# Row turns on the whole TensorE array and in other groups, and small tasks behind the score maxima, in a transformer block with an expert layer

## The chip, the cores and the metric

The kernel runs on one core of a Trainium2 chip. The metric is the device time of one execution in microseconds (us); of several executions the median is given.

A core has a matrix engine (TensorE, PE in the profile, with its weight loads shown as PEld), a vector engine (VectorE, DVE), a scalar engine (ScalarE, ACT), a general one (GpSimd, POOL) and one that here only issues transfers (SyncE, SP). Each works through its own list of instructions, and they wait for each other by semaphores. TensorE writes to a memory of its own, PSUM, from which VectorE and ScalarE take results ("evict" them).

## The reference

The input is 8 batches of 1,024 rows of 256 values. Cut to what matters:

```
h = layernorm(x) * (1 + ca) + sa
q, k, v = h @ w_qkv                 # 16 heads of 64
attn = softmax(q k^T / 8)           # over 1,024 keys, for each batch and head
x = x + ga * (concat(attn v) @ w_o)
h = layernorm(x) * (1 + cb) + sb
scores = softmax(h @ router_w + router_b)      # 8 experts
G, idx = top_k(scores.T, 512)                  # 512 rows for each expert
y[idx] += G * (relu(h[idx] @ w1 + b1) @ w2 + b2)
x = x + gb * y
```

The modulation vectors sa, ca, ga, sb, cb, gb come from a small product, one row for each batch. All is in 32-bit floating point.

## The kernel before

**Units and groups.** Attention is cut into 128 units. A unit is one batch, one pair of heads and one half (512) of the queries; there are 16 units in a batch. Its keys come in 8 chunks of 128. The main loop (line 732) runs over groups, numbered g, with two chunks of scores in each, so four groups make a unit and 64 make a batch. `gm = g % 4` is the place in the unit: first group (0) to last group (3).

**What a group does.** In order: loads that are due; in the second group the spreading of the previous unit's row maxima (`max_spread`); `subtract` on VectorE for two chunks of an earlier unit; for each of two chunks the scores (`scores_mm`, L367, two matmuls), a copy from PSUM by ScalarE (L376) and the running maximum on VectorE (L381); one small task, kind "m1"; VectorE and ScalarE tasks of kind "post"; the exponential on ScalarE (L429); the products with v for two chunks (`values_mm`, L438), which lag the scores by six groups; the sums of the exponentials on GpSimd (`add_up`, L454 and L457). In the last group of a unit there follow `max_turn` and `split_max`: eight transposes of the running maximum into PSUM (L388), a reduction (L396) and the splitting of the result into three short numbers (L401 to L404). Last come tasks of the kinds "pool" and "m2".

**Banks.** Scores have two PSUM buffers (pool `ps_s`), and the turned maximum takes one of the two until it is split. So the second chunk of scores in the next unit can't be written before L404 is done. Small tasks share one other buffer (`ps_m`).

**Small tasks.** Kind "m1" holds `qk_task` (L332), `v_task` (L349) and `max_rows` (L410). The first two make q, k and v for the next heads. Each of the second, third and last groups has about one of them, 1.8 us of TensorE each.

**Tasks around the attention.** `ln_task` prepares a later batch's rows, a quarter of a batch at a time: load, statistics on VectorE (`ln_stats`, L116 and L117), normalization on GpSimd (`ln_norm`, L281), and `ln_out`, which turns the rows by TensorE so that features lie across partitions, and evicts the turned rows with scale and shift. `out_load`, `out_proj` (L548) and `out_norm` (L571 to L573) do the output projection and the second normalization of the batch before, in eight parts; `out_turn` turns two parts, `out_route` (L600) makes the router's products, `out_exp` and `out_score` (L622 to L626) its softmax, `out_store` stores rows.

**Turns.** A turn of 256 rows by 256 features is four blocks of 128 by 128. Except in batch 0, `ln_out` makes each block of two matmuls with 64 columns of the rows as weights and the identity as data (L306), and so does `out_turn` (L585).

**Where tasks go.** There is no planner: `at(g, kind, ...)` puts a task into group g, and `run` takes it. `free_slot(g, True)` finds the next last group that has no such task yet; `free_slot(g)` the next second or third group. Both input turns, output turns and output projections thus stand in last groups, behind the maxima. By these calls a middle batch has, counted in groups from its start: projections in 7, 11, 19, 23, 31, 35, 59, 63; output turns in 3, 15, 27, 55; input turns in 39, 43, 47, 51. Batch 0 has only input turns, batch 1 has six projections and two output turns, and batch 7 ten and six.

**After the loop** the last batch's projection and routing follow, then the choice of rows for each expert by a search of the threshold, and the expert layer.

Of the kernel before, what the change touches and what calls it, by code (L numbers as in the profile page):

```python
# [31 lines left out]
AF = mybir.ActivationFunctionType  # L32
ALU = mybir.AluOpType
# [4 lines left out]
P = 128  # L38
# [4 lines left out]
def adaln_block(  # L43
# [15 lines left out]
    nc = tc.nc  # L59
    B, S, D = x.shape  # L60
    H, _, _, N = w_qkv.shape
    E, _, F = w1.shape
    K = 512
    KC = D // P
    NT = S // P
# [7 lines left out]
    scale = 1.0 / N**0.5  # L73
# [4 lines left out]
    ident = const.tile([P, P], F32, name="ident")  # L78
# [17 lines left out]
    modT = const.tile([P, 2 * KC, B], F32, name="modT")  # L96
# [36 lines left out]
    ps_m = attn.enter_context(tc.tile_pool(name="ps_m", bufs=1, space=PSUM))  # L133
# [33 lines left out]
    for i in range(2):  # L167
        t = work.tile([P, NT // 2, D], F32, tag="p", name=f"x_first{i}", bufs=PB)
# [73 lines left out]
    hTs, mods, qks, vs, oTs = {}, {}, {}, {}, {}  # L242
# [4 lines left out]
    def at(g, where, f, *args):  # L247
        steps.setdefault((g, where), []).append((f, args))

    def run(g, where):  # L250
        for f, args in steps.pop((g, where), ()):
            f(*args)
# [4 lines left out]
    def bank(shape, name, start=False):  # L257

        if start:
            return ps_s.tile(shape, F32, tag="s", name=name)  # L260
        return ps_m.tile(shape, F32, tag="mm", name=name)
# [24 lines left out]
    def ln_out(b, t):  # L286
        if t == 0:
            hTs[b] = work.tile([P, KC, S], F32, tag="hT", name=f"hT{b}")
        xt = ln_x.pop((b, t))[0]
        pt = bank([P, KC, 2 * P], f"ptx{b}_{t}", (b, t) in ((0, 0), (0, 1)))  # L290
        if b == 0:
            for k in range(KC):
                for i in range(2):
                    nc.tensor.transpose(
                        pt[:, k, i * P : (i + 1) * P], xt[:, i, k * P : (k + 1) * P], ident
                    )
                nc.scalar.activation(
                    hTs[b][:, k, 2 * t * P : (2 * t + 2) * P], pt[:, k, :], AF.Identity,
                    bias=modT[:, k, b : b + 1], scale=modT[:, KC + k, b : b + 1],
                )  # L300
            return
        for k in range(KC):
            for i in range(2):
                for m in range(2):
                    c0 = k * P + m * N
                    nc.tensor.matmul(  # L306
                        pt[m * N : (m + 1) * N, k, i * P : (i + 1) * P],
                        xt[:, i, c0 : c0 + N], ident, start=True, stop=True,
                    )
        for k in range(KC):  # L310
            nc.vector.tensor_scalar(
                hTs[b][:, k, 2 * t * P : (2 * t + 2) * P], pt[:, k, :],
                modT[:, KC + k, b : b + 1], modT[:, k, b : b + 1],
                op0=ALU.mult, op1=ALU.add,
            )

    def ln_task(b, t, g):
        at(g - 4, "load", ln_load, b, t)
        at(g - 2, "post", ln_stats, b, t)
        at(g - 1, "pool", ln_norm, b, t)  # L320
        at(g, "m2", ln_out, b, t)
# [70 lines left out]
    def split_max(u):  # L392

        tt = turned.pop(u)
        nm = tt[:, :2, :8]
        nc.vector.tensor_reduce(nm[:, 0, :], tt, AX.X, ALU.max, negate=True)  # L396
        part = [
            parts_of[u % 2][:, :, :, i].rearrange("p t j -> p j t") for i in range(3)
        ]
        whole, rest = (nm[:, i, :].rearrange("p (j t) -> p j t", j=2) for i in range(2))  # L400
        nc.vector.tensor_copy(part[0], whole)  # L401
        nc.vector.tensor_sub(rest, whole, part[0])
        nc.vector.tensor_copy(part[1], rest)
        nc.vector.tensor_sub(part[2], rest, part[1])  # L404
# [171 lines left out]
    def out_turn(pool, b, t, tag="mm"):  # L576

        n = f"{b}_{t}"
        pt = pool.tile([P, 2, KC, P], F32, tag=tag, name=f"pth{n}")
        for i in range(2):  # L580
            h2 = o_h[b, t + i]
            for k in range(KC):
                for m in range(2):
                    c0 = k * P + m * N
                    nc.tensor.matmul(  # L585
                        pt[m * N : (m + 1) * N, i, k, :], h2[:, c0 : c0 + N], ident,
                        start=True, stop=True,
                    )
        h2T = small.tile([P, 2, KC, P], F32, tag="h2T", name=f"h2T{n}", bufs=1)
        nc.scalar.copy(h2T, pt)  # L590
        o_x[b, t] = h2T
# [54 lines left out]
        )  # L646


    taken = set()

    def free_slot(g, behind=False):
        while g in taken or g % 4 == 0 or behind != (g % 4 == 3):
            g += 1
        taken.add(g)
        return g


    for t in range(NT // 2):
        at(-1 if t < 2 else 0, "m1", ln_out, 0, t)
        ln_task(1, t, free_slot(39 + 4 * t, True))  # L660
    for i, g in ((0, -1), (2, -1), (1, 0), (3, 1)):
        at(g, "m1", qk_task, 0, 0, i)
    for t, g in enumerate((1, 2, 3)):
# [1 line left out]
    for b in range(B):  # L665
        for p in range(NP):
            P0 = 8 * (b * NP + p)
            for i, g in enumerate((-7, -6, -5, -2)):
                if P0:
                    at(P0 + g, "m1", qk_task, b, p, i)  # L670
            if p % 2 == 0:
                for t, g in enumerate((-9, -3, -1, 5)):
                    if P0 or g > 0:
                        at(P0 + g, "m1", v_task, b, p // 2, t)
            if (b, p) == (B - 1, NP - 1):
                continue

            at(P0 + 17, "load", den_load, b, p)
            at(P0 + 18, "post", den_inv, b, p)
            at(P0 + 19, "load", den_spread, b, p)  # L680
            at(P0 + 20, "pool", den_mul, b, p)
        if b + 1 < B:
            if b + 2 < B:
                for t in range(NT // 2):
                    ln_task(b + 2, t, free_slot(64 * (b + 1) + 39 + 4 * t, True))
            for t in range(NT):
                g = free_slot(64 * (b + 1) + 19 + 4 * t, True)
                at(g - 2, "load", out_load, b, t)
                at(g, "m2", out_proj, ps_m, b, t)
                at(g + 1, "pool", out_norm, b, t)  # L690
                if t % 2:
                    g = free_slot(g + 2, True)
                    at(g, "m2", out_turn, ps_m, b, t - 1)
                    g = free_slot(g + 1)
                    at(g, "m2", out_route, ps_m, b, t - 1)
                    at(g + 1, "post", out_exp, b, t - 1)
                    at(g + 2, "post", out_score, b, t - 1)
                    at(g + 3, "pool", out_store, b, t - 1)
    for u in range(NSU):
        at(4 * u + 4, "m1", max_rows, u)  # L700
        if u < NSU - 1:
# [8 lines left out]
    with tc.manual_schedule():  # L710
# [20 lines left out]
        g = -1  # L731
        while g < 4 * NSU + LAG or steps:
            u, gm = divmod(g, 4)
            run(g, "load")
            if gm == 1 and 0 < u <= NSU:
                max_spread(u - 1)
            u1, gm1 = divmod(g - LAG + 1, 4)
            late = [(u1, 2 * gm1 + i) for i in range(2) if 0 <= u1 < NSU]

            for uc in late[: 1 if gm == 3 else 2]:  # L740
                subtract(*uc)
            if 0 <= u < NSU:
                for c in (2 * gm, 2 * gm + 1):
                    scores_out(u, c, scores_mm(u, c))
            if gm == 3 and late:
                subtract(*late[1])
            run(g, "m1")
            run(g, "post")
            for uc in late:
                exp_of(*uc)  # L750
            u1, gm1 = divmod(g - LAG, 4)
            if 0 <= u1 < NSU:
                for c in (2 * gm1, 2 * gm1 + 1):
                    values_mm(u1, c)
                    if u1 == NSU - 1:
                        if c == 0:
                            pd_last = ps_s.tile([P, QH], F32, tag="s", name="pd_last")
                        den_mm(pd_last, probs.pop((u1, c)), start=(c == 0), stop=(c == NT - 1))
                if gm1 == 3:
                    values_out(u1)  # L760
                if u1 < NSU - 1:
                    add_up(u1, gm1)
            if gm == 3 and 0 <= u < NSU:
                max_turn(u)
                split_max(u)
            run(g, "pool")
            run(g, "m2")
            g += 1


        b = B - 1
# [82 lines left out]
    with tc.tile_pool(name="search", bufs=2) as se, tc.tile_pool(  # L854
# [4 lines left out]
        for dst, pattern, mult in (  # L859
# [3 lines left out]
            i = po_.tile(list(dst.shape), I32, name=f"i_{dst.name}")  # L863
# [29 lines left out]
        for s in range(15):  # L893
            bit = 28 - 2 * s
            cnt = se.tile([P, 3], F32, tag="cnt", name=f"cnt{s}")
            for k in range(3):
# [3 lines left out]
                    op0=ALU.is_ge, op1=ALU.add, accum_out=cnt[:, k : k + 1],  # L900
# [209 lines left out]
```

## Time and profile before

| | |
|---|---|
| median of 3 runs | 3617.36 us (3617.17 to 3618.96) |
| the profiled execution | 3616.66 us |
| its span, first to last instruction | 3614.9 us |
| attention, batch 0 to batch 7 | 22 to 3185 us |
| tail of attention, search, experts | 3185 to 3615 us |
| busy in one middle batch of 398 us: PE, DVE, ACT, POOL | 396.2, 340.8, 298.4, 325.6 us |

A line of a group or of a timeline gives the engine, the line of the kernel, the operation, what it writes and reads with shapes, and a count. In a timeline the first two numbers are the start and the length in us from the start of the span, neighbouring instructions of one kind are merged (x8), and square brackets hold the idle time before it and what ended that. On TensorE an fp32 matmul is two instructions, and the ends of matmuls are modelled, so starts are the safer reading.

### The profile page before, as it was taken

To read this page: it belongs to the slowest core of one execution; us is meant where nothing else is said; L and a number is where in the kernel's file an instruction comes from. 1 tells how busy PE (TensorE), PEld (TensorE's weight loads), DVE (VectorE), ACT (ScalarE), POOL (GpSimd) and SP (SyncE) were. 2 spreads that over 40 slices of the span, in tenths; PEclk is the share of its full clock that TensorE was granted. 3 is DMA by queue.
4 is the path that set the end of the run, shared out by engine and by line. 5 is a ranking of instruction groups with operands and counts; after the bars stand their busy time and mean duration, and the time that the engine had idled before them with its cause. 6 is when DMAs were issued, how large, how long until landed. Compare 5 with 4: busy or idle time off the path is not lost. (4 is left out here: it accounts for less than half of the span.)

```text
span 3614.9 us, 54207 instructions
## 1 busy us (share of the span) xinstructions
PE 3458.4 (96%) x20622; PEld 1456.3 (40%) x20622; DVE 2898.9 (80%) x3641; ACT 2439.8 (67%) x2988; POOL 2660.0 (74%) x1537
## 2 busy tenths in 40 slices
PE   7999999999999999999999999999999999982898
PEld 3333333343433443344433434334334344342565
DVE  5888888888888888888888888888888888857442
ACT  4777777777777777777777777777777777730111
POOL 2778777887788887977888788877888877851332
PEclk9999999999999999999999999999999999995999
DMA  3010012011111113111211112011201112133332
GB/s 77 13 42 31 25 32 67 29 45 45 59 50 35 51 49 64 31 39 51 61 46 44 41 44 62 30 52 48 67 29 45 45 59 49 51 87 121 94 100 41
DMA packets 189652, 185.39 MB, mean 51 GB/s; under 512 B 48952, under 2 KB 167240, under 8 KB 189264
## 3 DMA queue, kind: packets, MB, share of 16 engines
q1 hardware_dynamic: 173616, 160.29, 15.5%
q0 software_dynamic: 7168, 12.72, 1.7%
q10 hardware_dynamic: 8608, 8.92, 0.8%
q8 instruction: 162, 2.65, 0.3%
q14 instruction: 98, 0.80, 0.1%
HBM read 127.06 MB, written 63.21 MB: 53 GB/s over the span
## 5 line engine op out<-in xcount | busy, mean ns | idle before, releaser
L457 POOL TENSOR_TENSOR acc<-acc,p 128x1024 f32<-128x1024 f32 x762 | 1806.6, 2371 | 361.2 <-ACT p L429 328.1
L376 ACT COPY p<-s 128x1024 f32<-128x1024 f32 x1024 | 997.2, 1020 | 417.8 <-PE s L367 407.7
L426 DVE TENSOR_TENSOR p<-p,less 128x1024 f32<-128x1024 f32 x1024 | 1206.8, 1210 | 32.5 <-PE less L423 30.0
L381 DVE TENSOR_TENSOR top<-top,s 128x1024 f32<-128x1024 f32 x768 | 936.9, 1220 | 276.5 <-ACT p L376 236.2
L429 ACT ACTIVATE p<-p 128x1024 f32<-128x1024 f32 x1024 | 1042.8, 1058 | 73.7 <-DVE p L426 73.4
L367 PE MATMUL s<-qk,qk 64*128 64x512 f32 x4096 | 1025.1, 612 | 34.0 <-DVE parts L404 31.0
L438 PE MATMUL av<-p,v 128*64 128x512 f32 x4096 | 967.1, 593 | 1.8 <-ACT oT L447 1.8
L367 PEld LDWEIGHTS s<-qk,qk 64*128 64x128 f32 x4096 | 358.7, 186 | 527.8 <-issue 241.2
L332 PE MATMUL pq<-hT,wq 128*64 128x512 f32 x2048 | 498.4, 608 | 2.7 <-ACT v L354 2.1
L438 PEld LDWEIGHTS av<-p,v 128*64 128x64 f32 x4096 | 280.5, 137 | 461.4 <-issue 366.2
L454 POOL TENSOR_TENSOR acc<-p,p 128x1024 f32<-128x1024 f32 x127 | 301.8, 2376 | 178.0 <-ACT p L429 178.0
L332 PEld LDWEIGHTS pq<-hT,wq 128*64 128x64 f32 x2048 | 124.8, 136 | 342.4 <-issue 210.8
L349 PE MATMUL pv<-wq,hT 128*64 128x256 f32 x2048 | 249.3, 385 | 0.7 <-ACT qk L337 0.7
L1035 ACT ACTIVATE h<-ph,b_sb 128x512 f32<-128x512 f32 x64 | 44.1, 689 | 274.7 <-PE ph L1031 274.7
L396 DVE TENSOR_REDUCE tt<-tt 128x8 f32<-128x1024 f32 x128 | 157.4, 1230 | 69.6 <-PE tt L388 69.5
L548 PE MATMUL po<-wo,ot 128*64 128x256 f32 x1792 | 205.7, 382 | 0.0
L349 PEld LDWEIGHTS pv<-wq,hT 128*64 128x64 f32 x2048 | 135.6, 136 | 153.3 <-issue 65.9
L381 DVE TENSOR_TENSOR top<-p,s 128x1024 f32<-128x1024 f32 x128 | 155.8, 1217 | 14.5 <-ACT p L376 14.5
L388 PEld LDWEIGHTS tt<-ident,top 128*128 128x128 f32 x1024 | 109.6, 140 | 106.6 <-DVE top L381 105.8
L519 POOL TENSOR_TENSOR oT<-oT,rb 128x1024 f32<-128x1024 f32 x63 | 150.1, 2382 | 3.0 <-DMA rb<-rden_d 3.0
L548 PEld LDWEIGHTS po<-wo,ot 128*64 128x64 f32 x1792 | 123.6, 137 | 66.1 <-issue 9.4
L388 PE MATMUL tt<-ident,top 128*128 128x128 f32 x1024 | 139.9, 280 | 2.6 <-DVE top L381 2.6
(166 smaller groups left out, 2357.3 us busy)
## 6 DMA issues: line engine op xcount, KB each, us to landing
rb<-rden_d SPq DMA_DIRECT2D x128, 256.0 KB
oT_d<-oT SPq DMA_DIRECT2D x62, 512.0 KB
ot<-oT_d SPq DMA_DIRECT2D x56, 512.0 KB
rows_d<-row SPq DMA_DIRECT2D x64, 132.0 KB
rows_d<-gb_d SPq DMA_DIRECT2D x8, 1024.0 KB
w<-in_L_ffn_w_dram ACTq DMA_DIRECT2D x8, 1024.0 KB
w<-in_L_ffn_w_dram SPq DMA_DIRECT2D x8, 1024.0 KB
lnx<-in_L_attn_inputs_dram SPq DMA_DIRECT2D x28, 256.0 KB
```

Source lines behind the costliest of these rows:

```text
L332: nc.tensor.matmul(pq[m * N : (m + 1) * N, :], wq_of(k, a, 2 * p + m), hTs[b][:, k, sl], start=(k == 0), stop=(k == KC - 1),)
L349: nc.tensor.matmul(pv[m * N : (m + 1) * N, i, :], hTs[b][:, k, t0 : t0 + N], wq_of(k, 2, 4 * g, 4), start=(k == 0), stop=(k == KC - 1),)
L367: nc.tensor.matmul(ps[:, j, :], kt[r, c * P : (c + 1) * P], qt[r, h * QB : (h + 1) * QB], start=True, stop=True,)
L376: nc.scalar.copy(probs[u, c], ps)
L381: nc.vector.tensor_tensor(tops[u], probs[u, 0] if c == 1 else tops[u], ps, ALU.max)
L388: nc.tensor.transpose(turned[u][:, 4 * j + t, :], top[:, j, t * P : (t + 1) * P], ident)
L426: nc.vector.tensor_tensor(probs[u, c], probs[u, c], less[u], ALU.add)
L429: nc.scalar.activation(probs[u, c], probs[u, c], AF.Exp)
L438: nc.tensor.matmul(avs[u][j * N : (j + 1) * N, :], v[:, c, hh * N : (hh + 1) * N], pT[:, j, :], start=(c == 0), stop=(c == NT - 1),)
L454: nc.gpsimd.tensor_tensor(sums[u], pts[0], pts[1], ALU.add)
L457: nc.gpsimd.tensor_tensor(sums[u], sums[u], pt, ALU.add)
L548: nc.tensor.matmul(po[m * N : (m + 1) * N, :], ot[:, p, m * N : (m + 1) * N], wo[:, p, :], start=(p == 0), stop=(p == NP - 1),)
```

## The change

There are three parts.

1. **Turns.** `ln_out` and `out_turn` make each 128 by 128 block by one `transpose` on the whole array. In `ln_out` all four come first and then two evictions, by ScalarE, for every batch. (Before, batch 0 had transposes, interleaved with evictions by ScalarE; the others had half-array matmuls and evictions by VectorE.)
2. **Places.** `free_slot` goes. Counted in groups of a batch, input turns now stand in 30, 34, 42 and 46 and output turns in 26, 38, 50 and 62: all third groups. Projections stand in 19, 23, 31, 35, 43, 47, 55 and 59, last groups. The output turn comes 3 groups after its second projection, the router's products after 6, its exponential after 7, its softmax's end after 9, the store after 10. Input rows are prepared for the next batch, with load, statistics and normalization 4, 2 and 1 groups ahead of their turn as before, which is now one batch number lower in the formula and the same batch in effect.
3. **Last groups without an output projection.** There the small task ("m1") runs after the maxima are turned and split, not before.

```diff
@@ ln_out
-        if b == 0:
-            for k in range(KC):
-                for i in range(2):
-                    nc.tensor.transpose(
-                        pt[:, k, i * P : (i + 1) * P], xt[:, i, k * P : (k + 1) * P], ident
-                    )
-                nc.scalar.activation(
...
-            return
         for k in range(KC):
             for i in range(2):
-                for m in range(2):
-                    c0 = k * P + m * N
-                    nc.tensor.matmul(
-                        pt[m * N : (m + 1) * N, k, i * P : (i + 1) * P],
-                        xt[:, i, c0 : c0 + N], ident, start=True, stop=True,
-                    )
+                nc.tensor.transpose(
+                    pt[:, k, i * P : (i + 1) * P], xt[:, i, k * P : (k + 1) * P], ident
+                )
         for k in range(KC):
-            nc.vector.tensor_scalar(
-                hTs[b][:, k, 2 * t * P : (2 * t + 2) * P], pt[:, k, :],
-                modT[:, KC + k, b : b + 1], modT[:, k, b : b + 1],
-                op0=ALU.mult, op1=ALU.add,
+            nc.scalar.activation(
+                hTs[b][:, k, 2 * t * P : (2 * t + 2) * P], pt[:, k, :], AF.Identity,
+                bias=modT[:, k, b : b + 1], scale=modT[:, KC + k, b : b + 1],
             )
@@ out_turn
-                for m in range(2):
-                    c0 = k * P + m * N
-                    nc.tensor.matmul(
-                        pt[m * N : (m + 1) * N, i, k, :], h2[:, c0 : c0 + N], ident,
-                        start=True, stop=True,
-                    )
+                nc.tensor.transpose(pt[:, i, k, :], h2[:, k * P : (k + 1) * P], ident)
@@ places
-        ln_task(1, t, free_slot(39 + 4 * t, True))
...
-            if b + 2 < B:
-                for t in range(NT // 2):
-                    ln_task(b + 2, t, free_slot(64 * (b + 1) + 39 + 4 * t, True))
+            for t in range(NT // 2):
+                ln_task(b + 1, t, 64 * b + (30, 34, 42, 46)[t])
             for t in range(NT):
-                g = free_slot(64 * (b + 1) + 19 + 4 * t, True)
+                g = 64 * (b + 1) + 19 + 4 * (t + t // 2)
+                covered.add(g)
                 at(g - 2, "load", out_load, b, t)
                 at(g, "m2", out_proj, ps_m, b, t)
                 at(g + 1, "pool", out_norm, b, t)
                 if t % 2:
-                    g = free_slot(g + 2, True)
-                    at(g, "m2", out_turn, ps_m, b, t - 1)
-                    g = free_slot(g + 1)
-                    at(g, "m2", out_route, ps_m, b, t - 1)
-                    at(g + 1, "post", out_exp, b, t - 1)
-                    at(g + 2, "post", out_score, b, t - 1)
-                    at(g + 3, "pool", out_store, b, t - 1)
+                    at(g + 3, "m2", out_turn, ps_m, b, t - 1)
+                    at(g + 6, "m2", out_route, ps_m, b, t - 1)
+                    at(g + 7, "post", out_exp, b, t - 1)
+                    at(g + 9, "post", out_score, b, t - 1)
+                    at(g + 10, "pool", out_store, b, t - 1)
@@ main loop
-            run(g, "m1")
+
+            behind = gm == 3 and g not in covered
+            if not behind:
+                run(g, "m1")
             run(g, "post")
...
             if gm == 3 and 0 <= u < NSU:
                 max_turn(u)
                 split_max(u)
+            if behind:
+                run(g, "m1")
             run(g, "pool")
             run(g, "m2")
```

More of the change, by code (lines that the diff above doesn't have):

```diff
@@ L290, in ln_out @@
         pt = bank([P, KC, 2 * P], f"ptx{b}_{t}", (b, t) in ((0, 0), (0, 1)))
-        if b == 0:
-            for k in range(KC):
-                for i in range(2):
-                    nc.tensor.transpose(
-                        pt[:, k, i * P : (i + 1) * P], xt[:, i, k * P : (k + 1) * P], ident
-                    )
-                nc.scalar.activation(
-                    hTs[b][:, k, 2 * t * P : (2 * t + 2) * P], pt[:, k, :], AF.Identity,
-                    bias=modT[:, k, b : b + 1], scale=modT[:, KC + k, b : b + 1],
-                )
-            return
         for k in range(KC):
             for i in range(2):
-                for m in range(2):
-                    c0 = k * P + m * N
-                    nc.tensor.matmul(
-                        pt[m * N : (m + 1) * N, k, i * P : (i + 1) * P],
-                        xt[:, i, c0 : c0 + N], ident, start=True, stop=True,
-                    )
+                nc.tensor.transpose(
+                    pt[:, k, i * P : (i + 1) * P], xt[:, i, k * P : (k + 1) * P], ident
+                )
         for k in range(KC):
-            nc.vector.tensor_scalar(
-                hTs[b][:, k, 2 * t * P : (2 * t + 2) * P], pt[:, k, :],
-                modT[:, KC + k, b : b + 1], modT[:, k, b : b + 1],
-                op0=ALU.mult, op1=ALU.add,
+            nc.scalar.activation(
+                hTs[b][:, k, 2 * t * P : (2 * t + 2) * P], pt[:, k, :], AF.Identity,
+                bias=modT[:, k, b : b + 1], scale=modT[:, KC + k, b : b + 1],
             )
@@ L582, in out_turn @@
             for k in range(KC):
-                for m in range(2):
-                    c0 = k * P + m * N
-                    nc.tensor.matmul(
-                        pt[m * N : (m + 1) * N, i, k, :], h2[:, c0 : c0 + N], ident,
-                        start=True, stop=True,
-                    )
+                nc.tensor.transpose(pt[:, i, k, :], h2[:, k * P : (k + 1) * P], ident)
         h2T = small.tile([P, 2, KC, P], F32, tag="h2T", name=f"h2T{n}", bufs=1)
@@ L646, in last_load @@
         )
[L649 to L655, printed above, removed]
+    covered = set()
     for t in range(NT // 2):
         at(-1 if t < 2 else 0, "m1", ln_out, 0, t)
-        ln_task(1, t, free_slot(39 + 4 * t, True))
     for i, g in ((0, -1), (2, -1), (1, 0), (3, 1)):
```

## The prediction

> **What bounds the kernel now.** First the page: TensorE (PE) is busy 96% of the span. Then the table of busy time by stretch: a full batch takes 398 us and PE is busy for 396 of them.
>
> ```profile
> PE 3458.4 (96%) x20622; PEld 1456.3 (40%) x20622; DVE 2898.9 (80%) x3641; ACT 2439.8 (67%) x2988; POOL 2660.0 (74%) x1537
> ```
>
> The columns of the stretch are its bounds and length, then busy time (and instructions) of PE, its weight loads, VectorE (DVE), ScalarE (ACT) and GpSimd (POOL), the granted clock, the DMA share and GB/s:
>
> ```profile
> 1603.00:2001.00 398.00, 396.22 (x2402) 159.09 (x2400) 340.75 (x409) 298.35 (x364) 325.61 (x184) 1.00 0.16 47
> ```
>
> Ends of matmuls are modelled, so I read starts. First PE's timeline of a last group (g%4 = 3, here g%64 = 27) with a turn behind the maxima, and the start of the next group:
>
> ```profile
> 575.42 1.99 PE L367 MATMUL s<-qk,qk 64*128 64x512 f32 x8
> 577.34 1.94 PE L332 MATMUL pq<-hT,wq 128*64 128x512 f32 x8
> 579.11 1.89 PE L438 MATMUL av<-p,v 128*64 128x512 f32 x8
> 580.92 1.09 PE L388 MATMUL tt<-ident,top 128*128 128x128 f32 x8
> 581.95 1.09 PE L585 MATMUL pth<-ident,row 128*64 128x128 f32 x16
> 582.97 1.13 PE L367 MATMUL s<-qk,qk 64*128 64x512 f32 x4
> 584.32 1.13 PE L367 MATMUL s<-qk,qk 64*128 64x512 f32 x4 [0.23 <-DVE parts L404]
> ...
> 588.24 1.88 PE L367 MATMUL s<-qk,qk 64*128 64x512 f32 x8
> ```
>
> Counted from 575.42, in us: scores 0, small task (m1) 1.92, values 3.69, maxima 5.50, turn 6.53, first new scores 7.55, second 8.90, next group 12.82. The second new scores wait: one of the two score banks holds the maxima until VectorE has split them. A last group of batch 1 with nothing behind the maxima has the wait much longer, and the same end: 428.87 to 441.69 is again 12.82.
>
> ```profile
> 435.40 1.13 PE L367 MATMUL s<-qk,qk 64*128 64x512 f32 x4
> 437.77 1.13 PE L367 MATMUL s<-qk,qk 64*128 64x512 f32 x4 [1.25 <-DVE parts L404]
> ```
>
> So a turn in that place is free today: it fills a wait. A group with an output projection behind the maxima (1793.56) has no wait: next scores at 10.14, next group at 14.92. Elsewhere PE has no holes: every third group (g%4 = 2) takes 5.50, the sum of its parts.
>
> What sets the wait is VectorE. Its timeline in the first of these groups, and at the end of batch 7, in a last group that has no small task ahead of the maxima:
>
> ```profile
> 577.70 2.55 DVE L381 TENSOR_TENSOR top<-top,s 128x1024 f32<-128x1024 f32 x2 [1.68 <-ACT p L376]
> 583.99 0.19 DVE L404 TENSOR_TENSOR parts<-tt,parts 128x8 bf16<-128x8 f32 x1
> ...
> 3187.55 2.54 DVE L381 TENSOR_TENSOR top<-top,s 128x1024 f32<-128x1024 f32 x2
> ```
>
> And PE in that group of batch 7:
>
> ```profile
> 3190.14 1.09 PE L388 MATMUL tt<-ident,top 128*128 128x128 f32 x8 [0.59 <-DVE top L381]
> ```
>
> The running maximum is done at 580.25 (4.83 on that count): it follows from the scores by way of ScalarE's copies and two maxima in a row. The maxima's transposes start 0.05 after it where PE is waiting (3190.14 against 3190.09). The parts are done 3.26 after their start (584.18 - 580.92), and scores follow 0.14 later.
>
> **What the skill says.** The Trainium skill, "TensorEngine Tiling (Array Packing)", Restrictions: column tiling disables transpose mode for FP32. The trace agrees: half-array turns are plain matmuls with two instructions each (L585: 16 for 8), L388 has one per transpose. "TensorE: Matmul & The Clock Gate", Part 4: a transpose took about 275 ns in a kernel; here L388 has a median of 273 ns, but issues every 0.129 us (8 in 1.03, 580.92 to 581.95). "PSUM — Partial Sum Buffer", Engine vs sequencer instructions: VectorE, ScalarE and GpSimd queues are strict FIFO; so a late operation delays all behind it. "SBUF — State Buffer", Who interferes with whom: VectorE and GpSimd share a port pair under an exclusive lock. L626 shows it: 0.22 us each, but 1.7 to 2.0 where an L457 of GpSimd is running, ending with it.
>
> **The change, part by part.**
>
> 1. Whole-array turns. 16 instructions took 1.02 us (581.95 to 582.97); 4 transposes at 0.129 take 0.515. But they move from last groups, where the 1.02 cost nothing, to third groups, where PE is full. Seven batches with 4 turns of normalized input and 4 of attention output: 56 x 0.515 = **+28.8 us**. Batch 7's own four output turns stay in the tail.
>
> 2. The small task behind the maxima. There are 128 last groups, 56 with projection in both versions (only spread differently); 72 others. The last has no small task; take one more as lost at the start: 70. PE now comes to the maxima at 5.50 - 1.77 = 3.73 and waits until 4.83 + 0.05 = 4.88. Then maxima to 5.91, small task 1.77 to 7.68 (first new scores), the second at 7.68 + 0.96 = 8.64; parts are ready at 4.88 + 3.26 + 0.14 = 8.28, so no wait. Next group at 7.68 + 4.78 (the unstalled first group: 1803.70 to 1808.48) = 12.46, against 12.82: 70 x 0.36 = **-25.2 us**. The cover changes sides: 1.15 us of wait stand ahead of the maxima instead. The small task's eviction now comes behind both exponentials on ScalarE; it ends about 8.5, the next copy starts about 8.9. Its bank is free before the row maxima use it (about 9.6). Its reader comes groups later.
>
> 3. Statistics and scores move into first groups. Statistics were in g%64 = 37, 41, 45, 49; now 28, 32, 40, 44. Router scores were in last groups under a projection (31, 59, 7, 19); now 32, 44, 56, 4. So 32 and 44, both right after a projection, get both. VectorE there, today:
>
> ```profile
> 1807.54 1.21 DVE L381 TENSOR_TENSOR top<-p,s 128x1024 f32<-128x1024 f32 x1
> 1808.75 2.35 DVE L426 TENSOR_TENSOR p<-p,less 128x1024 f32<-128x1024 f32 x2
> 1811.02 2.54 DVE L381 TENSOR_TENSOR top<-top,s 128x1024 f32<-128x1024 f32 x2
> 1813.48 2.35 DVE L426 TENSOR_TENSOR p<-p,less 128x1024 f32<-128x1024 f32 x2
> ```
>
> And GpSimd:
>
> ```profile
> 1808.54 0.73 POOL L573 TENSOR_TENSOR row<-row,mod 128x256 f32<-128x256 f32 x1
> ```
>
> The new work goes in at 1808.75. Statistics delay what follows by 1.09 (1839.28 to 1840.37), scores by about 0.9 if L626 gets the port when L573 ends at 1809.27: it would ask near 1809.1. Together 2.0. The second pair's maximum, done 1813.56, frees the bank for scores on PE at 1814.83: slack 1.27 less 0.05. Stall 2.0 - 1.2 = 0.8, in batches 1 to 6 twice: 12 x 0.8 = **+9.6 us**. Statistics alone, or scores alone, fit: after an unprojected last group VectorE idles 0.7 there and has 1.7 of slack.
>
> 4. Evictions of the normalized turn: two of VectorE (536 ns) become two of ScalarE (569). ScalarE has them ahead of the copies of a projected last group, whose maximum ends about 0.5 later, 5.35, still under 5.50. I take 0.1 for the bank in 12 groups: +1. If that cover were gone, each 0.1 of lateness is 2.8 us.
>
> 5. GpSimd: normalization (3.7 us) follows the other normalization and the divide in 44 and 45; it ends about when PE turns in 46. DMA: input loads at 26, 30, 38, 42 on SyncE, with two buffers long free; projection loads spread wider; nothing queued behind them is due within two groups. Start and tail: fewer waits of turns on evictions, about -1.
>
> Sum: 28.8 - 25.2 + 9.6 + 1 - 1 = +13. The profiled execution took 3616.66 (span 3614.9); the median is 0.7 above. 3617.4 + 13 = 3630.6; I say **3631**.
>
> Bounds of what the trace does not show: the gain in 2 lies between 0.2 (maxima start 0.15 later) and 0.45 per group, so -14 to -31; a turn of 4 cannot be under 4 x 0.129 nor, if it cost like today's, over 1.02 (+28); the stall in 3 between 0 and 3.2 (next rival).
>
> **Rivals.**
>
> *VectorE swallows the extra work* (0.27): nothing from 3; +3.6 in all, 3621. For it: slack of 1.2 to 1.7 us in each such place. Against: 2.0 are to be hidden.
>
> *The port lock is missed* (0.10): L626 asks after GpSimd has begun the next 2.37 us addition. Then 32 and 44 lose 3.2 each (38 instead of 9.6) and 56 loses 2.0 seven times (14): about 3673. For it: margin of only 0.15 us; against: where L626 waits today it gets in at the very next boundary.
>
> *Faster* (0.08): the maxima start sooner than 4.88 once the small task is gone. It decides below 4.73: then 70 groups gain over 0.51 each, 36 us, and with 3's stall absorbed the sum passes -7; just beyond that point the time is 3609. With no wait at all (maxima at 3.73) it would be 70 x 1.15 = 80 us under 3621, about 3541, the far end. For it: PE does come 1.15 sooner. Against: copies and maxima run without a gap from the scores on, and batch 7's group shows PE waiting for them.
>
> *Turns as dear as today* (0.04): that whole-array turning saves nothing. +28 more, 3659; L388 speaks against.
>
> **How the numbers follow.** My forecast has 0.51, 3625 to 3645. About 0.2% (7 us) is what a measurement of this kernel can tell from no change. The forecast lies nearly all beyond it; the swallowing rival within, some of its upper side beyond. Slower 0.67, same 0.25, faster 0.08. Range 3617 to 3657: it leaves out faster, the missed lock, and the edges.
>
> **What would show it.** Third groups with a turn at about 6.02 instead of 5.50; turns with one instruction per transpose, PE busy about 28 us less; the wait of L367 for the parts (31.0 us) nearly gone and one of about 1.1 us ahead of the maxima in some 70 groups; next group at 12.46; the third group after 32 and 44 with scores waiting for the maximum. Wrong if the maxima start off 4.88, or if L626 grows to 2 us in first groups.

## The result, and the profile after

The changed kernel takes 3700.65 us (median of 6 runs, 3698.47 to 3703.08) against 3617.69 us before: 83 us more, a ratio of 1.023 with a 95% interval of 1.022 to 1.0241. The prediction was 3631 us, slower, in a range up to 3657. The direction was right, and the size was six times too small.

The profiled execution of the changed kernel took 3703.08 us, its span is 3701.1 us. The page's line of busy time, and the stretch of batch 3 (columns as in the prediction: bounds, length, PE, weight loads, VectorE, ScalarE, GpSimd, clock, DMA share, GB/s):

```profile
PE 3454.1 (93%) x19902; PEld 1428.6 (39%) x19902; DVE 2894.3 (78%) x3585; ACT 2460.9 (66%) x3044; POOL 2658.4 (72%) x1537
```

```profile
1234.27:1644.40 410.13, 395.22 (x2304) 155.38 (x2304) 340.01 (x401) 301.64 (x372) 325.24 (x184) 1.00 0.16 46
```

A batch has gone from 398 to 410 us. PE has 720 instructions fewer and hardly less busy time; nearly all that was added stands as waiting. This is a last group without projection (g%64 = 27), the counterpart of the one in the prediction, on PE's timeline:

```profile
1400.26 0.66 PE L568 MATMUL pth<-ident,row 128*128 128x128 f32 x4
1400.85 1.99 PE L352 MATMUL s<-qk,qk 64*128 64x512 f32 x8
1402.77 1.94 PE L423 MATMUL av<-p,v 128*64 128x512 f32 x8
1405.73 1.09 PE L373 MATMUL tt<-ident,top 128*128 128x128 f32 x8 [1.02 <-DVE top L366]
1406.75 1.94 PE L317 MATMUL pq<-hT,wq 128*64 128x512 f32 x8
1408.62 1.99 PE L352 MATMUL s<-qk,qk 64*128 64x512 f32 x8
...
1413.40 1.88 PE L352 MATMUL s<-qk,qk 64*128 64x512 f32 x8
```

The turn now stands at the end of the third group and takes 0.59 us (1400.26 to 1400.85). The maxima start 4.88 after the scores, just where the prediction put them. New scores start at 7.77, and the next group at 12.55 (1413.40 - 1400.85), where it was 12.82. The second new scores no longer wait. The list of waits has the exchange, before and then after:

```profile
PE s L367 <- DVE parts L404: 31.0, 70, 1.3
```

```profile
PE tt L373 <- DVE top L366: 77.2, 74, 2.8
PE s L352 <- DVE top L366: 46.1, 53, 2.8
```

The columns are us in all, times, and the longest. The first line of after is the expected wait ahead of the maxima. The second is where the prediction failed: scores that wait for VectorE to finish the running maximum, 46.1 us by this list. It is found in few places. This is PE around group 33 of batch 3, the second group after a projection:

```profile
1440.22 1.88 PE L352 MATMUL s<-qk,qk 64*128 64x512 f32 x8
1442.03 1.94 PE L317 MATMUL pq<-hT,wq 128*64 128x512 f32 x8
1443.80 1.89 PE L423 MATMUL av<-p,v 128*64 128x512 f32 x8
1447.86 1.13 PE L352 MATMUL s<-qk,qk 64*128 64x512 f32 x4 [2.17 <-DVE top L366]
1449.18 1.13 PE L352 MATMUL s<-qk,qk 64*128 64x512 f32 x4 [0.20 <-DVE top L366]
```

VectorE's timeline just ahead of that wait, and GpSimd's:

```profile
1439.28 1.22 DVE L366 TENSOR_TENSOR top<-p,s 128x1024 f32<-128x1024 f32 x1
1440.41 0.16 DVE L602 TENSOR_REDUCE rd<-ex 128x2 f32<-128x16 f32 x1
1440.61 0.17 DVE L603 RECIPROCAL rd<-rd 128x2 f32<-128x2 f32 x1
1440.81 0.23 DVE L606 TENSOR_SCALAR row<-ex,rd 128x8 f32<-128x8 f32 x1
...
1440.95 2.40 DVE L606 TENSOR_SCALAR row<-ex,rd 128x8 f32<-128x8 f32 x1
1443.27 0.41 DVE L116 BATCH_NORM_STATS2 st_a<-lnx 128x6 f32<-128x256 f32 x1
...
1446.59 2.54 DVE L366 TENSOR_TENSOR top<-top,s 128x1024 f32<-128x1024 f32 x2
```

```profile
1440.28 0.73 POOL L558 TENSOR_TENSOR row<-row,mod 128x256 f32<-128x256 f32 x1
1440.97 4.81 POOL L442 TENSOR_TENSOR acc<-acc,p 128x1024 f32<-128x1024 f32 x2
```

There are two multiplications at L606, one for each of two row tiles. The first starts at 1440.81 and is through at 1441.04, as GpSimd's L558 ends at 1441.01. GpSimd's next instruction is an addition (two of some 2.4 us are merged in the line above). It starts at 1440.97, and the second multiplication of 8 columns takes 2.40 us: it ends with that addition. Everything behind it on VectorE, the statistics, two subtractions and two maxima, comes 2.3 us later than I had reckoned, and PE stands for 2.17 us. It is alike in groups 32, 44 and 56 of every batch (in 44 the GpSimd instruction that the second waits for is the multiplication L504). In group 4 the first multiplication asks as an addition begins and takes 2.40 us, and the second passes with it.

The long wait has a second price. In batch 3, after the same wait in group 45, the granted clock of PE falls. Its timeline and the stretches:

```profile
1527.82 1.13 PE L352 MATMUL s<-qk,qk 64*128 64x512 f32 x4 [2.16 <-DVE top L366]
1529.15 2.08 PE L352 MATMUL s<-qk,qk 64*128 64x512 f32 x4 [0.20 <-DVE top L366]
1531.15 2.54 PE L317 MATMUL pq<-hT,wq 128*64 128x512 f32 x8
```

```profile
1520.00:1526.00 6.00, 5.66 (x38) 2.37 (x34) 5.86 (x11) 4.19 (x7) 5.84 (x5) 1.00 0.29 104
1526.00:1530.00 4.00, 1.98 (x6) 0.80 (x8) 3.90 (x4) 3.07 (x4) 3.72 (x6) 0.87 0.73 212
1530.00:1533.00 3.00, 3.00 (x10) 0.67 (x8) 2.90 (x4) 1.08 (x2) 3.00 (x3) 0.60 0.00 0
1533.00:1539.00 6.00, 6.00 (x36) 2.47 (x34) 2.74 (x3) 5.24 (x7) 4.77 (x3) 1.00 0.00 0
```

The clock (the number ahead of the DMA share) is below 1.00 in the two middle rows. The four score instructions of the second chunk take 2.08 us, where 1.13 is usual.

### The profile page after: what moved, and what is told of

It is laid out like the page before. It is cut to its first block, busy times and chain, and to the rows that moved or that the text cites. A ratio compares the mean times of both kernels' runs of the same rounds, so it can differ in the third digit from the quotient of the medians.

```text
span 3701.1 us, 52878 instructions
## 1 busy us (share of the span) xinstructions
PE 3454.1 (93%) x19902; PEld 1428.6 (39%) x19902; DVE 2894.3 (78%) x3585; ACT 2460.9 (66%) x3044; POOL 2658.4 (72%) x1537
## 5 line engine op out<-in xcount | busy, mean ns | idle before, releaser
L442 POOL TENSOR_TENSOR acc<-acc,p 128x1024 f32<-128x1024 f32 x762 | 1804.7, 2368 | 462.9 <-ACT p L414 429.2
L352 PE MATMUL s<-qk,qk 64*128 64x512 f32 x4096 | 1022.6, 616 | 46.9 <-DVE top L366 46.1
L317 PE MATMUL pq<-hT,wq 128*64 128x512 f32 x2048 | 505.9, 616 | 3.8 <-ACT v L339 2.1
L373 PE MATMUL tt<-ident,top 128*128 128x128 f32 x1024 | 139.9, 280 | 77.2 <-DVE top L366 77.2
L504 POOL TENSOR_TENSOR oT<-oT,rb 128x1024 f32<-128x1024 f32 x63 | 149.5, 2373 | 8.8 <-DMA rb<-rden_d 8.8
```

What stands on the lines that cost most here:

```text
L317: nc.tensor.matmul(pq[m * N : (m + 1) * N, :], wq_of(k, a, 2 * p + m), hTs[b][:, k, sl], start=(k == 0), stop=(k == KC - 1),)
L352: nc.tensor.matmul(ps[:, j, :], kt[r, c * P : (c + 1) * P], qt[r, h * QB : (h + 1) * QB], start=True, stop=True,)
L373: nc.tensor.transpose(turned[u][:, 4 * j + t, :], top[:, j, t * P : (t + 1) * P], ident)
L442: nc.gpsimd.tensor_tensor(sums[u], sums[u], pt, ALU.add)
```

## The sum that the trace gives

Durations of groups are differences of the starts of their scores. Each of these is a place in the changed kernel compared with the same kind of group without a stall.

| part | working | us |
|---|---|---|
| turns in third groups | 56 x 0.59 | +33 |
| small task behind the maxima | 70 x 0.27 (12.55 for 12.82) | -19 |
| stalls in groups 33, 34 and 45, 46 | 14.7 + 9.4 + 14.7 + 10.7 | +49.5 |
| stalls in groups 57, 58 and 5, 6 | 8.2 + 3.7 + 3.2 + 2.8 | +18 |
| first groups of batch 0 | start and unit 0 | +4 |
| sum | | +85.5 |

The spans of the two profiled executions differ by 86.2. The stalls of the third row follow the scores' end and the statistics together in batches 1 to 6; batch 7 prepares no rows, and there, after the scores' end alone, groups 33 and 45 lose 1.2 instead of 2.25. Those of the fourth row follow the scores' end alone. Of the +49.5, some 13 is the halved clock: groups 34 and 46 of batches 1 to 6 take 6.56 without it and up to 8.2 with it. In batch 0 the small task behind the maxima is both a v and a q/k task in group 3, before values keep PE busy.

## The experiments

Two theories stood for the stalls. **P** (port): a multiplication waits for GpSimd to finish an addition. **W** (work): first groups hold too much VectorE work, whatever each operation waits for.

**No port.** The multiplication in the form that also sums its output, same engine, same place:

```diff
-            nc.vector.tensor_scalar_mul(row[:, D:], ex[:, i, :], den[:, i : i + 1])
+            one = small.tile([P, 1], F32, tag="one", name=f"one{n}_{i}", bufs=1)
+            nc.vector.tensor_scalar(
+                row[:, D:], ex[:, i, :], den[:, i : i + 1], 0.0,
+                op0=ALU.mult, op1=ALU.add, accum_out=one,
+            )
```

> The changed kernel with one edit: the two score multiplications of out_score are done by VectorE in the form that also writes an accumulator, in the same place; nothing is left out. Theory P (port): the second multiplication waits a whole GpSimd addition (2.3 us) for the shared port, in all of groups 33, 45, 57 and 5's predecessors; if that form doesn't take the port, the scores cost about 0.9 us instead of 3.1, the stalls after 56 and 4 go (16 us), those after 32 and 44 fall to about 0.8 each (50 to 10 us): about 3645 us. Theory W (work): it is the amount of work moved into first groups, statistics and scores together, whatever each waits for: 3690 us or more.

Measured: 3646.68 us, ratio to before 1.008 (1.005 to 1.0109). P holds: of the 67 us of stalls in the table, 54 go with a change of form alone, and W can explain no more than what stays. VectorE's and GpSimd's timelines in group 32 of batch 3 of this kernel:

```profile
1422.90 0.22 DVE L607 TENSOR_SCALAR_CACHE_REDUCE row<-ex,rd 128x8 f32<-128x8 f32 x1
1423.04 0.08 DVE L607 DVE_READ_ACCUMULATOR row<-ex,rd 128x1 f32 x1
1423.16 0.22 DVE L607 TENSOR_SCALAR_CACHE_REDUCE row<-ex,rd 128x8 f32<-128x8 f32 x1
...
1423.31 0.42 DVE L116 BATCH_NORM_STATS2 st_a<-lnx 128x6 f32<-128x256 f32 x1
```

```profile
1423.07 4.83 POOL L442 TENSOR_TENSOR acc<-acc,p 128x1024 f32<-128x1024 f32 x2
```

The second multiplication now takes 0.22 us while the addition runs. The scores' end takes 0.8 from first operation to last. Groups 5, 6, 57 and 58 have no stall, 33 and 34 together 0.68, 45 and 46 some 0.9: about the 0.8 of the prediction's step 3. No half clock is recorded between batches 1 and 6. The Trainium skill says the same of the port ("SBUF — State Buffer", Who interferes with whom): it names tensor_scalar, except the form that writes out its accumulator, as able to take the shared pair. This run shows the exception at work.

**Statistics late.** The statistics of the input rows one group later, so in second groups:

```diff
-        at(g - 2, "post", ln_stats, b, t)
+        at(g - 1, "post", ln_stats, b, t)
```

> The changed kernel with the statistics of the input rows one group later, in second groups, the scores left where they are. Theory P: 33 and 45 then stall like 57 does now (1.7 us with the third group after it, no halved clock), and so do 57 and 5 as before: 29 us less, about 3672 us. Theory W: without the statistics the first groups hold no more than there is room for, all stalls go: about 3640 us. If the statistics were harmless: 3700 us.

Measured: 3678.55 us (1.0168, 1.0138 to 1.0197), 22 us less where P said 29 and W 60. The stall of group 33 is halved but not gone:

```profile
1435.25 1.13 PE L352 MATMUL s<-qk,qk 64*128 64x512 f32 x4 [1.13 <-DVE top L366]
```

So the scores alone, with their wait, still stall four groups a batch: 33, 45 and 57 take 6.58 for 5.39, group 5 takes 5.92 for 5.39, and each third group behind them 0.47 more. No halved clock is recorded from batch 1 to batch 7.

**Scores in last groups again.**

```diff
-                    at(g + 9, "post", out_score, b, t - 1)
-                    at(g + 10, "pool", out_store, b, t - 1)
+                    at(g + 8, "post", out_score, b, t - 1)
+                    at(g + 9, "pool", out_store, b, t - 1)
```

> The changed kernel with the end of the router's softmax one group earlier, that is in last groups again, three of four under an output projection, the fourth (group 3) in a last group without one. Theory P: the wait for the port is hidden by the projection again; statistics alone don't stall; the fourth holds up the splitting of the maxima by up to 2 us: 66 us less, 0 to 13 more, so 3635 to 3648 us. Theory W: the same where the statistics alone fit; if they don't, 33 and 45 keep stalls of 1 us or more, 3650 to 3665 us.

Measured: 3644.59 us (1.0074, 1.0045 to 1.0103). The wait for the port is still there (two multiplications in 1.61 us in group 31), but the projection on PE covers it. Groups 33 and 45 take 5.39 with statistics alone. The fourth place, group 3 without projection, costs 1.4 in the group after it.

**Statistics first.** Same groups, order turned round, so that both multiplications come while GpSimd's addition is running:

```diff
-        at(g - 2, "post", ln_stats, b, t)
+        at(g - 2, "stats", ln_stats, b, t)
...
+            run(g, "stats")
             run(g, "post")
```

> The changed kernel with the statistics ahead of the scores' end in groups 32 and 44, nothing else. Theory P in detail: in the changed kernel the first multiplication comes just as GpSimd's multiplication by the modulation ends and gets the port; GpSimd then starts an addition, and the second waits all of it. With the statistics first, both multiplications come 1.1 us later, while that addition runs, wait for its end together and pass together: the scores take some 1.7 us from their first operation instead of 2.9, the stalls of 33 and 45 shrink by 0.8 or more (12 times) and with them the halved clock goes (13 us): about 3677 us. If each multiplication waits for an addition of its own wherever it stands: 3700 us or more.

Measured: 3699.16 us (1.0227, 1.0197 to 1.0257): 22 us more than expected. In group 32 it went as expected: both multiplications took 1.64 us, and the stall of group 33 is 1.33 for 2.25. In group 44 they took 3.82, and the stall of group 45 grew to 3.5. VectorE's and GpSimd's timelines in 44:

```profile
1518.78 2.40 DVE L606 TENSOR_SCALAR row<-ex,rd 128x8 f32<-128x8 f32 x1
```

```profile
1516.47 2.37 POOL L504 TENSOR_TENSOR oT<-oT,rb 128x1024 f32<-128x1024 f32 x1
1518.80 4.80 POOL L442 TENSOR_TENSOR acc<-acc,p 128x1024 f32<-128x1024 f32 x2
```

The first passed when L504 ended at 1518.84; L442 was already under way, and the second waited for all of its first addition. Between two additions in a row, GpSimd starts 0.08 after the end of the one before, and there the second multiplication slips in; L442 starts 0.04 before the end of L504, and there it doesn't. The traces of the ten kernels that have this form of multiplication agree: the second waited in all 78 places where GpSimd's next instruction overlapped the one before, by 0.04 to 0.06, and passed in all 222 where it started 0.08 after it. That the gap decides is still a reading; it wasn't tried by itself.

**Task ahead.** The third part of the change undone:

```diff
-            behind = gm == 3 and g not in covered
+            behind = False
```

> The changed kernel with the small task ahead of the maxima in every last group, as before. Step 2 of the prediction (the order helps, by 0.27 us for each of 70 groups as the trace of the changed kernel shows): 19 us more, about 3720 us, with the wait for the parts back at some 1.5 us and next group at 12.82. Rival (the new wait ahead of the maxima, 77 us in the list of waits, is what made the kernel slower): 40 us or more less, under 3660 us.

Measured: 3717.96 us (1.0277, 1.0247 to 1.0306), 17 more than the changed kernel. Last groups are back at 6.53 and their successors at 6.30 (12.83). So the new wait of 77.2 us ahead of the maxima is not a loss: it replaces a longer one, 87.5 us for the parts in this run's list of waits.

**Turns alone, in their old places.** The kernel before with whole-array turns and ScalarE's evictions, no task moved. The edit in `out_turn` is shown; `ln_out` has the one of the change.

```diff
-                for m in range(2):
-                    c0 = k * P + m * N
-                    nc.tensor.matmul(
-                        pt[m * N : (m + 1) * N, i, k, :], h2[:, c0 : c0 + N], ident,
...
+                nc.tensor.transpose(pt[:, i, k, :], h2[:, k * P : (k + 1) * P], ident)
```

> The kernel before with part 1 alone: whole-array turns, evicted by ScalarE, in their old places in last groups; nothing is left out. Step 1's claim that a turn behind the maxima fills a wait and costs nothing: halving it saves nothing either, PE is busy some 28 us less and waits that much more for the parts, 3617 us within 4. Rival (turns cost PE time wherever they stand): 28 us less, about 3590 us.

Measured: 3613.63 us, ratio 0.9992 (0.9983 to 1.0001): no difference that can be told. PE's timeline in group 27:

```profile
1374.27 1.09 PE L373 MATMUL tt<-ident,top 128*128 128x128 f32 x8
1375.19 0.60 PE L568 MATMUL pth<-ident,row 128*128 128x128 f32 x4
1375.72 1.13 PE L352 MATMUL s<-qk,qk 64*128 64x512 f32 x4
1377.67 0.70 PE L352 MATMUL s<-qk,qk 64*128 64x512 f32 x2 [0.81 <-DVE parts L389]
```

New scores start 6.96 after the group's start instead of 7.55, and the wait for the parts is longer by as much (0.81 for 0.23). In this place a turn is free at either length.

**Task behind, alone.** The kernel before with the third part only; `covered` holds the groups of its projections.

```diff
+            behind = gm == 3 and g not in covered
+            if not behind:
+                run(g, "m1")
...
+            if behind:
+                run(g, "m1")
             run(g, "pool")
```

> The kernel before with part 3 alone: the small task behind the maxima in last groups without projection, half-array turns still in last groups and after the small task. There PE waits ahead of the maxima and has small task and turn after them: next group at 12.55 + 1.02 = 13.57 against 12.82 in 56 groups, 12.55 in some 14: 38 us more, about 3656 us. If the wait ahead of the maxima could be hidden by a later cover: 3617 us.

Measured: 3701.6 us (1.0234, 1.0213 to 1.0254), 45 more than expected. The timeline shows what the expectation left out:

```profile
1406.50 1.09 PE L388 MATMUL tt<-ident,top 128*128 128x128 f32 x8 [1.02 <-DVE top L381]
1407.52 1.94 PE L332 MATMUL pq<-hT,wq 128*64 128x512 f32 x8
1410.16 1.09 PE L585 MATMUL pth<-ident,row 128*64 128x128 f32 x16 [0.70 <-ACT qk L337]
1411.18 1.99 PE L367 MATMUL s<-qk,qk 64*128 64x512 f32 x8
```

Small task and turn share one PSUM buffer. With nothing between them, the turn comes 0.77 later, waiting for the task's eviction. A last group and its successor take 14.34 instead of 12.82.

**The change without its stalls.** Changed kernel; statistics at `g - 1`, scores' end at `g + 8` (the fourth at `g + 24`, under a projection too) with the store a group behind it, small task of group 3 ahead. Two of the edits:

```diff
-                    at(g + 9, "post", out_score, b, t - 1)
+                    at(g + (8 if t < 7 else 24), "post", out_score, b, t - 1)
...
-            behind = gm == 3 and g not in covered
+            behind = gm == 3 and g > 4 and g not in covered
```

> The changed kernel with its turns in third groups as they are, but with the scores' end under projections, the statistics in second groups and the small task of group 3 ahead again: what is left is step 1 (56 turns in third groups at 0.59 as seen there, +33) and step 2 (70 groups at 0.27, -19): 14 us over before, about 3632 us. If more hides in the move than these two: 3640 us or more.

Measured: 3633.18 us (1.0045, 1.0029 to 1.0061). Steps 1 and 2 add up to within 2 us of it. In the trace two smaller terms nearly cancel: the first two groups of batch 0 are 2.7 us shorter than before, and in batches 1 to 6 groups 46, 48 and 49 take 0.85 us longer together, 5 us in all. Most of that is the turn of group 46, which waits for GpSimd's normalization (L281):

```profile
1500.95 0.55 PE L293 MATMUL ptx<-ident,lnx 128*128 128x128 f32 x3 [0.34 <-POOL lnx L281]
```

**Turns in the idle time.** On top of that, all turns go to last groups without projection, ahead of the maxima, right after the scores. Input turns stand in groups 3, 7, 11, 15 of a batch (11, 15, 19, 23 in batch 0), output turns in 27, 39, 51, 63.

```diff
-                ln_task(b + 1, t, 64 * b + (30, 34, 42, 46)[t])
+                ln_task(b + 1, t, 64 * b + ((3, 7, 11, 15) if b else (11, 15, 19, 23))[t])
...
-                    at(g + 3, "m2", out_turn, ps_m, b, t - 1)
+                    at(g + 4, "turn", out_turn, ps_m, b, t - 1)
...
+            run(g, "turn")
             if not behind:
                 run(g, "m1")
```

(`ln_out` is of the kind "turn" as well; statistics and normalization both come two groups ahead of it.)

> The changed kernel rearranged: whole-array turns stand in last groups without a projection, right after the scores and ahead of the maxima, where PE waits 1.15 us; the small task stays behind the maxima (not in group 3); the scores end under projections (the fourth one 16 groups later), statistics in second groups. If the wait ahead of the maxima is real idle time, the turns (0.59 us) are free there, next group stays at 12.55 against 12.82, 19 us less than before: about 3599 us. Rival (the turn's eviction holds up ScalarE's copies and so the maxima): the maxima start 0.3 or more later than 4.88 and the gain is gone, 3617 us or more.

Measured: 3596.3 us, ratio to before 0.9942 (0.9926 to 0.9959). It beats both kernels, by 21 us the one before. PE in group 27 of batch 3:

```profile
1359.03 1.99 PE L352 MATMUL s<-qk,qk 64*128 64x512 f32 x8
1360.95 0.66 PE L568 MATMUL pth<-ident,row 128*128 128x128 f32 x4
1361.54 1.94 PE L423 MATMUL av<-p,v 128*64 128x512 f32 x8
1363.91 1.09 PE L373 MATMUL tt<-ident,top 128*128 128x128 f32 x8 [0.44 <-DVE top L366]
...
1371.58 1.88 PE L352 MATMUL s<-qk,qk 64*128 64x512 f32 x8
```

The maxima still start at 4.88 (1363.91 - 1359.03) and the next group at 12.55. The turn takes its 0.59 from the wait. Some 0.56 us of waiting is left in each of the 56 groups with a turn.

## Why the prediction was right and where it failed

**Step 1, turns:** right in kind; a turn cost 0.59 where I took 0.515, +33 for +28.8. I had counted only the mean pitch of transposes in a row (0.129). In the trace of the changed kernel the starts of the four stand 0.17, 0.11 and 0.11 apart, and the scores follow 0.20 after the last. That a turn behind the maxima was free in the kernel before was right: the run with turns in place shows it.

**Step 2, the small task:** right. The maxima start at 4.88, as reckoned; the gain was 0.27 per group for 0.36, since new scores came at 7.77 for 7.68: the small task takes 1.87 behind the maxima, 1.77 ahead of them. Group 3 of batch 0, for which I had left out the gain, cost 3.7 us instead (12.93 for 9.25).

**Step 3, VectorE in first groups:** this is the step that failed. It said: "scores by about 0.9 if L626 gets the port when L573 ends at 1809.27: it would ask near 1809.1". It did get the port there, within 0.03 us. But there are two multiplications. From the trace of before, where the second always passed with the first, I took it that both pass at one boundary. This is VectorE there, and GpSimd:

```profile
1724.06 2.13 DVE L626 TENSOR_SCALAR row<-ex,rd 128x8 f32<-128x8 f32 x2
```

```profile
1723.67 4.80 POOL L457 TENSOR_TENSOR acc<-acc,p 128x1024 f32<-128x1024 f32 x2 [0.57 <-ACT p L429]
```

The first waited through one addition, another addition followed 0.08 us after it, and the second multiplication went in between. In the changed kernel the first came just at the end of a GpSimd instruction and did not wait. The next GpSimd instruction had started 0.04 us before that end, and the second multiplication waited for all of it: 2.40 us for 0.22. So the rival "the port lock is missed" holds, by another door than the one I gave it; I gave it 0.10. Its size was wrong too: it had 3.2 for groups 32 and 44 (2.7 measured without the clock), 2.0 for 56 (1.65), and nothing for 4, which lost 1.0. Batch 7's groups 33 and 45 (1.7 each with the groups behind them) weren't in it either. The halved clock, about 13 us, was in no case of mine.

With the port taken out by the form of the multiplication, the same kernel takes 3646.68 us, and the stalls are those of step 3. The other 16 us over 3631 are a turn's 0.07 and the task's 0.09, which make 10, batch 0's 4, and the rest in the stalls, 11 us in all for the 9.6 reckoned.

**Steps 4 and 5:** in the changed kernel no separate wait for them shows. In group 31, after an input turn and the router's exponential, the running maximum ends at 5.07 instead of 4.83, still under 5.50. But the wait that step 5 put at nothing, the turn of group 46 for GpSimd's normalization, was only hidden by the stalls: in the run without them it costs 0.56 us in each of six batches.

Of the signs named: the third groups with a turn (6.09 for 6.02), the exchanged wait, and the scores that wait for the maximum were all found. So was one of the two signs of being wrong, L626 growing to 2 us in first groups: it is L606 in the changed kernel, 2.40 us. PE's busy time fell by 4 us, not by 28; in the run without the stalls it fell by 29.5, to 3428.9 us, so some 25 us of what the changed kernel shows as busy come with the stalls.

## What to carry to other kernels

Before moving a task out of a wait that it fills, look for what the place that it goes to is short of: here turns went from idle PE time to full groups, and a port wait went from under a projection to where VectorE had 1.2 us to spare. Where one engine shares a port under a lock, count every instruction that asks for it, one by one; here an operation of 0.22 us could cost the partner's whole instruction, 2.40 us, and another form of it did not wait at all. When a task is moved across a wait, look at what comes behind it in its new place and which buffer they share: the small task behind the maxima gained 19 us where no turn stood behind it, lost 84 where half-array turns came next and needed its buffer, and with whole-array turns in the gap that it had opened the kernel gained 21.

## What the hardware showed that I had not expected

- Two short VectorE multiplications in a row don't always keep the port between them: in groups 32, 44 and 56 the first took 0.23 us, then GpSimd's next instruction went in, and the second took 2.40. Where GpSimd left 0.08 us between two instructions, as in group 4 and in the kernel before, the second passed in 0.22.
- PE waits of 2.2 us were followed by a granted clock of 0.5 for 3.4 us, in nine of the twelve places of groups 33 and 45 in batches 1 to 6; why the other three escaped is open. With the statistics first, where group 45 stalls for 3.5 us, all six batches have it. The kernel before, with waits for the parts up to 1.3 us, has no halved clock in that stage. The Trainium skill ("TensorE: Matmul & The Clock Gate", Why this matters for your kernels) speaks of idle gaps above about 3 us between bursts of matmuls; here 2.2 us, with 0.2 more one chunk later, were followed by the halved clock in nine of twelve places.
- A turn of four transposes costs 0.59 us between other work and 0.53 right behind the maxima's transposes, though half of a row of eight takes 0.51.
